# A two-layer graph attention kernel: new order of small steps inside a unit of layer 0, and a shorter reciprocal root

## The chip, the cores and the metric

The kernel runs on one core of a Trainium2 chip. The metric is the device time of one execution in microseconds, lower is better. The kernel before took 1904.17 us as the median of three runs (1901.87 to 1906.42). A profile is one further execution, recorded by the hardware profiler; it took 1750.29 us, and its span from the first to the last instruction is 1748.6 us.

## The reference, cut to what matters

There are 2708 nodes with 1024 features and a sparse 0/1 adjacency matrix (the diagonal is set). Layer 0 is a dot-product graph attention with weights Wf, Wg, W, layer 1 an additive one with W, a1, a2; each is followed by a residual sum and a layer norm.

```python
def _L0_gnn_ref(x, adj, Wf, bf, Wg, bg, W, bW):
    f = x @ Wf + bf
    g = x @ Wg + bg
    e = jax.nn.relu(f @ g.T)
    scores = jnp.where(adj > 0, e, NEG)
    attention = jax.nn.softmax(scores, axis=1)
    return attention @ (x @ W + bW)
...
x = _layernorm(x + _L0_gnn_ref(...))     # layer 0
x = _layernorm(x + _L1_gnn_ref(...))     # layer 1: relu(softmax(mask(leaky_relu(h a1 + (h a2)^T))) h), h = x W
```

## The kernel before, in words

A first stage turns the adjacency rows into lists of neighbours (up to 40 a node), written to the DRAM table `LD`, and multiplies the weights: `M` is the product of Wf and Wg transposed, so a score is a dot product between a neighbour's row of x and a row F = x M of the node itself.

Nodes are sorted by number of neighbours into groups of 32, and four groups make a *unit* of 128 nodes; layer 0 has 22 units (21 full ones and one of a single group). In a unit every group has its own number of tiles; a *tile* is 128 gathered rows of x, four neighbours for each of 32 nodes. Nearly all units have 20 tiles, the last three have 16, 16 and 15.

The ring (L868) has 20 slots of 128 rows. So the tiles of the next unit can be gathered only as the sums of this unit free their slots. Each gather is one indirect DMA on GpSimd's queue.

The loop over units (L1025) does, for unit u, with the work of its neighbours interleaved:

- On TensorE: the weighted sums of u (`lay.sums`, L712), `po` = softmax weights `st` times the gathered rows, then the row totals `pt`, one small matmul a group; transposes of a later unit's x rows (`x_turn`, L902); the product with W of the unit before (into `pm`, residual and norm follow); a small matmul that spreads q; the product F with M of the unit after next (`f_product`, L907); transposes of u's sums `y`.
- On ScalarE: `replicate` (L910) copies F of the next unit into four tiles `Fr`, one for each group, four copies each; the norm of `z` of the unit before; `y` = `po` times the reciprocal of the totals; copies of the transposed tiles.
- On VectorE: `dots` (L916), one dot product of a gathered tile with `Fr`, 20 in a unit, in an order that alternates between groups 0 and 1, then 2 and 3; `soft` (L921, L682), which adds q, masks, takes the maximum, has ScalarE take the exponential, and builds `st` and its row sums `rs`; the residual sum, statistics and root of the unit before (`close`, L932, and `norm`, L604); `q_dot` (L888), one dot of a later unit's x rows; two dots of the normed `z` for layer 1; the reciprocal `ri` of the totals.
- On GpSimd's queue: the 20 ring gathers as slots come free (`gathers`, L669), the scatter of the finished rows to the table of layer 1 (`T<-z`), the load of x rows for a later unit (`load_x`, `xb`), the load of the residual (`load_residual`, L926, into `z`), and four gathers of neighbour lists (`load_lists`, L857, `SL<-LD`) for the unit four ahead.

Each engine executes its instructions in the order in which the program issues them: the class `InOrder` (L61) wraps every engine and binds each instruction behind the one before. That is why almost every line of the profile is L71, the wrapper's line, and why groups are told apart by tile names. Between engines, waits follow from the tiles.

Buffers that matter: `z` (L874), `xb`, `y` and `po` have one buffer, so `z` can be loaded again only when the scatter has read it; transposes and small matmuls share two PSUM buffers `pt` (`ps_t`, L138), so the second of the two x transposes waits until the totals have been read by the reciprocal; products share two buffers `pm`.

`closing` is the generator `close` of the unit before. Its first step (residual sum, statistics, root, shift `sh`) is issued at the end of an iteration, behind `soft` of the next unit. In the next iteration come ScalarE's norm of `z` and its store (second step), the two dots of `z` (third step), and, behind the sums, the scatter. The reciprocal stands at the end of `lay.sums`, so on VectorE it comes behind these dots.

Layer 1 gathers rows of the table T in the same way, in half units, with the same `norm`.

Of the kernel before, what the change touches and what calls it, by code (L numbers as in the profile page):

```python
# [18 lines left out]
EPS = 1e-5  # L19
# [87 lines left out]
def listed_path(ctx, tc, x, adj, Wf, bf, Wg, bg, W, bW, W1, a1, a2, out):  # L107
# [491 lines left out]
    def scatter(table, idx, src):  # L599
        pool.indirect_dma_start(  # L600
            out=table, out_offset=bass.IndirectOffsetOnAxis(ap=idx, axis=0), in_=src,
            in_offset=None, bounds_check=N - 1, oob_is_err=False)

    def norm(z, n, made=None):  # L604


        st = small.tile([P, H, 6], F32, name="bst")
        mv = small.tile([P, 2], F32, name="mv")
        for h in range(H):
            if made is not None:  # L610
                made(h)
            dve.bn_stats(st[:n, h, :], z[:n, h * 512:(h + 1) * 512])
        dve.bn_aggr(mv[:n], st[:n])
        var, r, t = (small.tile([P, 1], F32, name=s) for s in ("var", "rstd", "newton"))
        dve.tensor_scalar(var[:n], mv[:n, 1:2], EPS, None, op0=ALU.add)
        ri, ti = r.bitcast(I32), t.bitcast(I32)
        dve.tensor_scalar(ti[:n], var.bitcast(I32)[:n], 1, None, op0=ALU.logical_shift_right)
        dve.tensor_scalar(ri[:n], ti[:n], -1.0, float(0x5F3759DF), op0=ALU.mult, op1=ALU.add)
        for _ in range(3):
            dve.tensor_scalar(t[:n], var[:n], r[:n], r[:n], op0=ALU.mult, op1=ALU.mult)  # L620
            dve.tensor_scalar(t[:n], t[:n], -0.5, 1.5, op0=ALU.mult, op1=ALU.add)
            dve.tensor_scalar(r[:n], r[:n], t[:n], None, op0=ALU.mult)
        sh = small.tile([P, 1], F32, name="sh")
        dve.tensor_scalar(sh[:n], mv[:n, 0:1], r[:n], -1.0, op0=ALU.mult, op1=ALU.mult)
        yield
        act.activation(z[:n, :D], z[:n, :D], AF.Identity, bias=sh[:n], scale=r[:n])
# [24 lines left out]
    class Layer:  # L651
# [57 lines left out]
            u.rs = small.tile([P, Q], F32, name="rs")  # L709
            dve.tensor_reduce(u.rs[:, :u.G], sc, AX.X, ALU.add)  # L710

        def sums(self, u, po, y):  # L712

            place = lambda k, h: 32 * ((k + 2 * h) % 4)

            def totals():
                pt = ps_t.tile([P, 4, P], F32, name="pt")  # L720
                for h in range(H):
                    for k in range(u.G):
                        j = place(k, h)
                        pe.matmul(pt[j:j + 32, 0, h:h + 1], stack, u.rs[:, k:k + 1], start=True, stop=True)
                return pt

            index = {(k, t): m for m, (k, g, t) in enumerate(u.tiles)}

            queues = []
            for c in range(4):  # L730
                two = [(k, h) for h, k in enumerate((c, (c + 2) % 4)) if k < u.G]
                if c > 1:
                    two.reverse()
                queues.append([(k, h, t) for t in range(u.T) for k, h in two if t < TILES[u.gs[k]]])
            done, halves, pt = 0, {}, None
            while any(queues):
                if pt is None and done >= min(4, u.T):
                    pt = totals()
                now = [q.pop(0) for q in queues if q]
                for k, h, t in now:  # L740
                    j = place(k, h)
                    pe.matmul(po[j:j + 32, h, :], u.st[:, u.col[k, t], :],
                              self.rows(u.at + index[k, t])[:, h * 512:(h + 1) * 512],
                              start=(t == 0), stop=(t == TILES[u.gs[k]] - 1))
                for k, h, t in now:
                    halves[k, t] = halves.get((k, t), 0) + 1
                    if halves[k, t] == H:
                        self.free.add(u.at + index[k, t])
                        self.gathers()
                        done += 1  # L750
            if pt is None:
                pt = totals()
            ri = small.tile([P, H], F32, name="ri")
            spans = [(slice(0, P), slice(0, H))] if u.G == 4 else \
                [(slice(j, j + 32), slice(h, h + 1)) for h in range(H) for j in (place(0, h),)]
            for rows, h in spans:
                dve.reciprocal(ri[rows, h], pt[rows, 0, h])
            for h in range(H):
                rows = slice(0, P) if u.G == 4 else slice(place(0, h), place(0, h) + 32)
                c = slice(h * 512, (h + 1) * 512)  # L760
                act.activation(y[rows, c], po[rows, h, :], AF.Copy, scale=ri[rows, h:h + 1])
# [107 lines left out]
    with ExitStack() as s0s:  # L869
# [10 lines left out]
        def load_x(b):  # L880
            xb[b] = xp.tile([P, D], F32, name="xb") if b > 0 else zs[:, :D]
            gather(pool, xb[b][:nrows[b]], x, ids[:nrows[b], b:b + 1])
# [5 lines left out]
        def q_dot(b):  # L888
            n = nrows[b]
            qs = small.tile([P, 1], F32, name="qs")  # L890
            dot(xb[b][:n], rb, n, qs[:n])
            qd[b] = spread(qs[:n], n, "qd")
# [9 lines left out]
        def x_turn(b):  # L902
            xTs[b] = tp.tile([P, KC, P], F32, name="xT")
            for _ in turn(xb[b], nrows[b], xTs[b]):
                pass
# [4 lines left out]
        def replicate(b, k):  # L910

            Fr[b, k] = frp.tile([P, D], F32, name="Fr")
            for p in range(Q):
                act.copy(Fr[b, k][32 * p:32 * p + 32, :], flat(F[b])[32 * k:32 * k + 32, :])
# [106 lines left out]
        soft(units[0])  # L1021
        for _ in spread2:
            pass
        closing, loaded = iter(()), 3
        for k, u in enumerate(units):  # L1025
            nxt = units[k + 1] if k + 1 < len(units) else None
            b = u.b
            back = seq[k - 1] if k > 0 else None
            ahead = seq[k + 2] if k + 2 < NB else None

            first = k == 0
            po = ps_s.tile([P, H, 512], F32, name="po")
            y[b] = yp.tile([P, D], F32, name="y")
            if back is not None:
                for _ in yTs[back][1]:
                    pass
            reps = list(range(len(nxt.gs))) if nxt is not None and not first else []
            for r in reps[:1]:
                replicate(nxt.b, r)
            next(closing, None)  # L1040
            if loaded is not None:
                q_dot(loaded)
                loaded = None
            next(closing, None)
            for r in reps[1:3]:
                replicate(nxt.b, r)
            if nxt is None:

                for _ in closing:
                    pass  # L1050
                Wp[back] = product(P, yTs.pop(back)[0], Wt, 1)
            lay.sums(u, po, y[b])
            for _ in closing:
                pass
            closing = iter(())
            if ahead is not None and not first:
                x_turn(ahead)
            if k + 3 < NB and not first:
                loaded = seq[k + 3]
                load_x(loaded)  # L1060
            if back is not None and nxt is not None:
                load_residual(back)
                if back > 0:
                    Wp[back] = product(P, yTs.pop(back)[0], Wt, 1)
                else:
                    Wp[back] = whole(split_product(yTs.pop(back)[0], Wt, frp.tile([P, D], F32, name="Fr"), 1))
            if k + 2 == NB:
                load_residual(b)
            spreading = iter(())
            if ahead is not None and not first:  # L1070
                spreading = q_spread(ahead)
                next(spreading)
            for r in reps[3:]:
                replicate(nxt.b, r)
            if ahead is not None and not first:
                f_product(ahead)
            if ahead == NB - 1:
                sp.dma_start(M, W1.rearrange("(k p) d -> p k d", p=P))
            yT = tp.tile([P, KC, P], F32, name="xT")
            steps = turn(y[b], nrows[b], yT, halves=True)  # L1080
            next(steps)
            yTs[b] = yT, steps
            if k + 2 == NB:
                for _ in steps:
                    pass
            if k + 4 < NB and not first:
                load_lists(seq[k + 4])
            if nxt is not None:
                dots(nxt, 0, len(nxt.tiles))
            for _ in spreading:  # L1090
                pass
            if nxt is not None:
                soft(nxt)
            if back is not None:
                closing = close(back)
                next(closing)
# [529 lines left out]
```

## Time and profile before

| what | value |
|---|---|
| median of three runs | 1904.17 us |
| profiled execution | 1750.29 us |
| its span | 1748.6 us |
| 14 full units of layer 0, 405.36 to 975.97 us | 570.61 us |
| one dot of a tile on VectorE | 1.23 us |
| one ring gather on GpSimd's queue, issue | 1.06 us on average |
| one list gather, issue | 1.0 us |
| one replication of F (four copies) on ScalarE | 4.0 us |
| layer 1, from about 1140 us on | 608 us |

A profile line with a time in front is one instruction or several merged ones: start, duration, engine, line, operation, output and input tiles, shapes, count; the bracket is the idle time of the engine before it and what ended it. A line of waits has the engine and tile that waited, what it waited for, the total in us, how often, and the longest. Digits of a clock row are tenths of the full TensorE clock in 40 equal slices. A wait for several things is put down to the last event by time, which may be a chance neighbour.

### The profile page before, as it was taken

How to read it: one execution, taken by the hardware profiler on the slowest of the kernel's cores; microseconds unless marked ns; L12 is line 12 of the kernel's file. 1: busy time of each engine (PE TensorE's matmuls, PEld its weight loads, DVE VectorE, ACT ScalarE, POOL GpSimd, SP SyncE). 2: the span in 40 equal slices, each digit the busy share in tenths (PEclk: the TensorE clock that was granted, in tenths of full speed). 3: DMA queues.
4: the chain of work that ended last, by engine and by line, in shares of the span. 5: the costliest groups of instructions: out<-in, count | busy, mean ns of one | idle time of the engine just before them, and what ended most of it. 6: DMA issues, size and time to landing. Idle time of an engine off the chain costs nothing. (4 is left out here: it accounts for less than half of the span.)

```text
span 1748.6 us, 23112 instructions
## 1 busy us (share of the span) xinstructions
PE 1563.6 (89%) x6969; PEld 675.5 (39%) x6969; DVE 1297.5 (74%) x4262; ACT 643.5 (37%) x902; POOL 1180.9 (68%) x1195
## 2 busy tenths in 40 slices
PE   4999578899999999999999999559899888999896
PEld 2444233344444444444444444213344333343332
DVE  5879846899999989998999977547465555665652
ACT  4555455444444554555554444101111111111111
POOL 7888476467667767776677743177777777777740
PEclk8999778999999999999999999879999999999998
DMA  7656168578877777888887876399999999999960
GB/s 287 228 185 236 38 232 309 199 252 292 302 277 283 269 253 276 294 293 284 303 299 285 291 267 249 121 394 357 367 374 392 391 397 375 384 392 390 396 253 38
DMA packets 149986, 502.80 MB, mean 288 GB/s; under 512 B 32340, under 2 KB 32372, under 8 KB 147144
## 3 DMA queue, kind: packets, MB, share of 16 engines
q0 software_dynamic: 132032, 428.29, 66.2%
q1 hardware_dynamic: 10202, 55.72, 8.4%
q10 hardware_dynamic: 7618, 17.23, 2.7%
q8 instruction: 57, 0.93, 0.2%
q14 instruction: 77, 0.63, 0.1%
HBM read 509.64 MB, written 33.75 MB: 311 GB/s over the span
## 5 line engine op out<-in xcount | busy, mean ns | idle before, releaser
L71 POOL DMA_INDIRECT ring<-in_x_dram,SL x405 | 429.9, 1062 | 164.0 <-issue 70.0
L71 DVE SCALAR_TENSOR_TENSOR j<-ring,Fr 128x1024 bf16<-128x1024 f32 x402 | 493.9, 1229 | 41.1 <-DMA ring<-in_x_dram,SL 13.9
L71 PE MATMUL po<-ring,st 128*32 128x512 f32 x2616 | 324.4, 616 | 56.9 <-ACT y L71 32.5
L71 ACT COPY Fr<-pm 32x1024 f32<-32x1024 f32 (+2 forms) x353 | 340.6, 965 | 18.8 <-PE pm L71 14.1
L71 PE MATMUL pm<-M,yT 128*128 128x512 f32 (+1 forms) x704 | 313.3, 598 | 0.5 <-ACT yT L71 0.5
L71 PE MATMUL pm<-Wt,xT 128*128 128x512 f32 (+1 forms) x704 | 300.5, 599 | 4.7 <-DMA Wt<-in_L_gnn_W_dram 4.7
L71 POOL DMA_INDIRECT ring<-T,SL x249 | 247.0, 992 | 80.5 <-issue 66.3
L71 PE MATMUL pm<-M,xT 128*128 128x512 f32 x672 | 297.5, 601 | 0.0
L71 ACT ACTIVATE scores<-scores 128x12 f32<-128x12 f32 (+9 forms) x65 | 14.0, 216 | 631.6 <-DVE scores L71 631.6
L71 PEld LDWEIGHTS pm<-M,yT 128*128 128x128 f32 (+1 forms) x704 | 127.8, 186 | 185.0 <-issue 183.8
L71 PEld LDWEIGHTS pm<-Wt,xT 128*128 128x128 f32 (+1 forms) x704 | 131.0, 189 | 163.4 <-issue 154.6
L71 PEld LDWEIGHTS pm<-M,xT 128*128 128x128 f32 x672 | 130.2, 194 | 158.0 <-issue 155.1
L71 POOL DMA_INDIRECT more<-T,SL x156 | 154.6, 991 | 48.5 <-issue 43.8
L71 PEld LDWEIGHTS po<-ring,st 128*32 128x32 f32 x2616 | 95.9, 113 | 229.8 <-issue 174.0
L412 POOL TENSOR_TENSOR adj<-adj,iota 128x2708 f32<-128x2708 f32 (+3 forms) x23 | 130.6, 5685 | 22.7 <-ACT adj L71 22.6
L415 DVE MAX8 cand<-adj 128x8 f32<-128x136 f32 (+2 forms) x440 | 97.2, 285 | 37.4 <-POOL adj L412 37.4
L71 PE MATMUL pm<-halfT,WfT 128*128 128x512 f32 x256 | 114.1, 601 | 1.1 <-ACT WfT L71 1.1
L71 POOL DMA_INDIRECT SL<-LD,idq x85 | 86.4, 1016 | 25.8 <-issue 24.0
L71 PE MATMUL po<-more,st 128*32 128x512 f32 x624 | 82.4, 625 | 14.3 <-ACT y L71 14.3
L71 DVE TENSOR_SCALAR scores<-ring,f1q 128x4 f32<-128x4 f32 (+6 forms) x69 | 16.5, 245 | 104.1 <-DMA ring<-T,SL 93.1
L71 POOL DMA_INDIRECT z<-in_x_dram,ids x21 | 24.0, 1142 | 87.1 <-DVE j L71 36.4
L71 PEld LDWEIGHTS pm<-halfT,WfT 128*128 128x128 f32 x256 | 48.2, 193 | 58.0 <-issue 55.2
(214 smaller groups left out, 1539.5 us busy)
## 6 DMA issues: line engine op xcount, KB each, us to landing
adj<-in_adj_dram SPq DMA_DIRECT2D x21, 1354.0 KB, 5.8
X1S<-z SPq DMA_DIRECT2D x19, 512.0 KB, 5.2
ring<-in_x_dram,SL POOLq DMA_INDIRECT x405, 6.5
rows<-in_L_gnn_Wg_dram ACTq DMA_DIRECT2D x8, 512.0 KB, 4.4
rows<-in_L_gnn_Wf_dram ACTq DMA_DIRECT2D x8, 512.0 KB, 3.5
rows<-in_L_gnn_W_dram ACTq DMA_DIRECT2D x8, 512.0 KB, 6.1
Wt<-in_L_gnn_W_dram ACTq DMA_DIRECT2D x1, 4096.0 KB
M<-in_L_gnn_W_dram SPq DMA_DIRECT2D x1, 4096.0 KB
```

The costliest lines, as they stand in the source:

```text
L71: made = self.tc.keep_in_program_order(op(*args, **kwargs))
L412: nc.gpsimd.tensor_tensor(k[:n, cut], k[:n, cut], iota[:n, cut], op=ALU.mult)
L415: nc.vector.max(cand[:n, s, :], k[:n, s * SEG:min((s + 1) * SEG, N)])
```

## The change

Five edits, all in layer 0's loop except the first.

- The reciprocal square root of `norm` becomes a function `rsqrt`: the variance is halved on entry (with the small constant added in the same instruction), the first guess gets a negative sign, and each of the three Newton steps has two instructions instead of three. Both layers use it.
- In `sums`, the reciprocal is issued directly behind the matmuls of the totals, and then `aside()` is called, which issues the norm of `z`, its two dots and the second and third replication. Before, these stood ahead of the call of `sums` and the reciprocal at its end.
- `load_lists` moves from behind the transposes of `y` to between `load_x` and `load_residual`: on GpSimd's queue the four list gathers now come behind the `xb` load and ahead of the `z` load.
- `q_dot` of the loaded x rows moves from the next iteration (behind the residual sum and root) to the end of this one, ahead of the residual sum. The first one, `q_dot(3)`, is issued ahead of the loop.
- The last four dots of the next unit move behind the addition that finishes q of a later unit (`spreading`).

```diff
+    def rsqrt(v, n, scale):
+        half, r, t = (small.tile([P, 1], F32, name=s) for s in ("half", "rstd", "newton"))
+        dve.tensor_scalar(half[:n], v, 0.5 * scale, 0.5 * EPS, op0=ALU.mult, op1=ALU.add)
+        ri, ti = r.bitcast(I32), t.bitcast(I32)
+        dve.tensor_scalar(ti[:n], half.bitcast(I32)[:n], 1, None, op0=ALU.logical_shift_right)
+        dve.tensor_scalar(ri[:n], ti[:n], -1.0, float(0x5F3759DF - 0x400000 - (1 << 31)), op0=ALU.mult, op1=ALU.add)
+        for _ in range(3):
+            dve.tensor_scalar(t[:n], half[:n], r[:n], r[:n], op0=ALU.mult, op1=ALU.mult)
+            dve.tensor_scalar(r[:n], t[:n], 1.5, r[:n], op0=ALU.subtract, op1=ALU.mult)
+        return r
...
-        dve.tensor_scalar(var[:n], mv[:n, 1:2], EPS, None, op0=ALU.add)
...
-        for _ in range(3):
-            dve.tensor_scalar(t[:n], var[:n], r[:n], r[:n], op0=ALU.mult, op1=ALU.mult)
-            dve.tensor_scalar(t[:n], t[:n], -0.5, 1.5, op0=ALU.mult, op1=ALU.add)
-            dve.tensor_scalar(r[:n], r[:n], t[:n], None, op0=ALU.mult)
+        r = rsqrt(mv[:n, 1:2], n, 1.0)
...
             def totals():
...
-                return pt
+                spans = ...
+                for rows, h in spans:
+                    dve.reciprocal(ri[rows, h], pt[rows, 0, h])
+                aside()
...
-            for rows, h in spans:
-                dve.reciprocal(ri[rows, h], pt[rows, 0, h])
...
-            next(closing, None)
-            if loaded is not None:
-                q_dot(loaded)
-                loaded = None
-            next(closing, None)
-            for r in reps[1:3]:
-                replicate(nxt.b, r)
...
+            def aside():
+                next(closing, None)
+                next(closing, None)
+                for r in reps[1:3]:
+                    replicate(nxt.b, r)
+
+            lay.sums(u, po, y[b], aside)
...
                 load_x(loaded)
+            if k + 4 < NB and not first:
+                load_lists(seq[k + 4])
             if back is not None and nxt is not None:
                 load_residual(back)
...
-            if k + 4 < NB and not first:
-                load_lists(seq[k + 4])
             if nxt is not None:
-                dots(nxt, 0, len(nxt.tiles))
+                dots(nxt, 0, max(0, len(nxt.tiles) - 4))
             for _ in spreading:
                 pass
             if nxt is not None:
+                dots(nxt, max(0, len(nxt.tiles) - 4), len(nxt.tiles))
                 soft(nxt)
+            if loaded is not None:
+                q_dot(loaded)
+                loaded = None
             if back is not None:
                 closing = close(back)
                 next(closing)
```

More of the change, by code (lines that the diff above doesn't have):

```diff
@@ L613, in norm @@
         dve.bn_aggr(mv[:n], st[:n])
-        var, r, t = (small.tile([P, 1], F32, name=s) for s in ("var", "rstd", "newton"))
-        dve.tensor_scalar(var[:n], mv[:n, 1:2], EPS, None, op0=ALU.add)
-        ri, ti = r.bitcast(I32), t.bitcast(I32)
-        dve.tensor_scalar(ti[:n], var.bitcast(I32)[:n], 1, None, op0=ALU.logical_shift_right)
-        dve.tensor_scalar(ri[:n], ti[:n], -1.0, float(0x5F3759DF), op0=ALU.mult, op1=ALU.add)
-        for _ in range(3):
-            dve.tensor_scalar(t[:n], var[:n], r[:n], r[:n], op0=ALU.mult, op1=ALU.mult)
-            dve.tensor_scalar(t[:n], t[:n], -0.5, 1.5, op0=ALU.mult, op1=ALU.add)
-            dve.tensor_scalar(r[:n], r[:n], t[:n], None, op0=ALU.mult)
+        r = rsqrt(mv[:n, 1:2], n, 1.0)
         sh = small.tile([P, 1], F32, name="sh")
@@ L710, in soft, with sums @@
             dve.tensor_reduce(u.rs[:, :u.G], sc, AX.X, ALU.add)
-        def sums(self, u, po, y):
+        def sums(self, u, po, y, aside):
             place = lambda k, h: 32 * ((k + 2 * h) % 4)
+            ri = small.tile([P, H], F32, name="ri")
             def totals():
@@ L724, in totals @@
                         pe.matmul(pt[j:j + 32, 0, h:h + 1], stack, u.rs[:, k:k + 1], start=True, stop=True)
-                return pt
+                spans = [(slice(0, P), slice(0, H))] if u.G == 4 else \
+                    [(slice(j, j + 32), slice(h, h + 1)) for h in range(H) for j in (place(0, h),)]
+                for rows, h in spans:
+                    dve.reciprocal(ri[rows, h], pt[rows, 0, h])
+                aside()
             index = {(k, t): m for m, (k, g, t) in enumerate(u.tiles)}
@@ L734, in sums @@
                 queues.append([(k, h, t) for t in range(u.T) for k, h in two if t < TILES[u.gs[k]]])
-            done, halves, pt = 0, {}, None
+            done, halves, summed = 0, {}, False
             while any(queues):
-                if pt is None and done >= min(4, u.T):
-                    pt = totals()
+                if not summed and done >= min(4, u.T):
+                    summed = True
+                    totals()
                 now = [q.pop(0) for q in queues if q]
@@ L750, in sums @@
                         done += 1
[L751 to L755, printed above, removed]
-            for rows, h in spans:
-                dve.reciprocal(ri[rows, h], pt[rows, 0, h])
+            if not summed:
+                totals()
             for h in range(H):
@@ L1023, in listed_path @@
             pass
-        closing, loaded = iter(()), 3
+        closing = iter(())
+        q_dot(3)
         for k, u in enumerate(units):
@@ L1051, in listed_path @@
                 Wp[back] = product(P, yTs.pop(back)[0], Wt, 1)
-            lay.sums(u, po, y[b])
+            def aside():
[4 more added lines that the diff above has]
+            lay.sums(u, po, y[b], aside)
             for _ in closing:
@@ L1092, in listed_path @@
             if nxt is not None:
+                dots(nxt, max(0, len(nxt.tiles) - 4), len(nxt.tiles))
                 soft(nxt)
+            if loaded is not None:
+                q_dot(loaded)
+                loaded = None
             if back is not None:
```

## The prediction

> **What bounds the kernel now.** I read the page's clock row first, then busy time cut at successive starts of `st` (VectorE, once per unit), then the waits of each engine between 405.36 and 975.97 us, then the timeline of one unit.
>
> ```profile
> span 1748.6 us, 23112 instructions
> ...
> PE 1563.6 (89%) x6969; PEld 675.5 (39%) x6969; DVE 1297.5 (74%) x4262; ACT 643.5 (37%) x902; POOL 1180.9 (68%) x1195
> ...
> PEclk8999778999999999999999999879999999999998
> ```
>
> Busy time by unit (PE, PEld, DVE, ACT, POOL, clock, DMA share):
>
> ```profile
> 732.24:772.86 40.62, 39.62 (x186) 17.26 (x185) 37.15 (x82) 20.77 (x25) 28.74 (x28) 1.00 0.81 290
> 772.86:813.90 41.04, 39.95 (x187) 17.35 (x184) 37.28 (x83) 20.77 (x26) 28.74 (x28) 1.00 0.80 282
> 813.90:854.61 40.71, 38.69 (x177) 16.57 (x178) 37.35 (x82) 20.73 (x25) 27.32 (x28) 1.00 0.80 292
> ```
>
> The 14 units between 405.36 and 975.97 take 570.61 us, 40.76 us each, at full clock. TensorE and VectorE both look full. The waits tell which pays (us in total, times, longest):
>
> ```profile
> DVE j L71 <- DMA ring<-in_x_dram,SL: 11.4, 20, 1.2
> DVE z L71 <- DMA z<-in_x_dram,ids: 4.9, 11, 1.3
> DVE st L71 <- ACT scores L71: 4.3, 15, 0.3
> DVE j L71 <- ACT Fr L71: 4.2, 14, 0.3
> PE pt L71 <- DVE ri L71: 10.3, 12, 2.0
> PE po L71 <- DVE st L71: 5.1, 8, 1.0
> ```
>
> VectorE has no slack: 37.3 us recorded busy, 1.8 us of named waits per unit (24.8/14), and the rest is spacing between short instructions. TensorE waits 15.4/14 = 1.1 us per unit, always for VectorE. So VectorE's order is the loop that sets the unit. One unit on GpSimd, ScalarE, VectorE and TensorE:
>
> ```profile
> 804.23 1.02 POOL L71 DMA_INDIRECT T<-z,ids  x1 [0.30 <-issue]
> 805.55 1.03 POOL L71 DMA_INDIRECT xb<-in_x_dram,ids  x1 [0.30 <-issue]
> 810.96 0.99 POOL L71 DMA_INDIRECT z<-in_x_dram,ids  x1 [4.38 <-DVE q L71]
> 812.25 1.00 POOL L71 DMA_INDIRECT SL<-LD,idq  x1 [0.30 <-issue]
> ...
> 817.46 0.99 POOL L71 DMA_INDIRECT ring<-in_x_dram,SL  x1 [0.30 <-issue]
> ```
> ```profile
> 779.85 1.24 ACT L71 ACTIVATE z<-z,sh,rstd 128x1024 f32<-128x1024 f32 x1 [1.84 <-DVE sh L71]
> 781.11 8.12 ACT L71 COPY Fr<-pm 32x1024 f32<-32x1024 f32 x8
> ```
> ```profile
> 785.20 1.22 DVE L71 SCALAR_TENSOR_TENSOR j<-ring,Fr 128x1024 bf16<-128x1024 f32 x1 [0.31 <-ACT Fr L71]
> ```
> ```profile
> 783.76 0.66 PE L71 MATMUL pt<-ident,xb 128*128 128x128 f32 x4 [0.52 <-DVE ri L71]
> 1027.44 1.11 PE L71 MATMUL pt<-ident,xb 128*128 128x128 f32 x4 [3.14 <-DVE ri L71]
> ```
>
> GpSimd idles 4.38 us before `z`, then spends 5.2 us on lists, and only then refills the ring. ScalarE cannot make the second `Fr` before it has normed `z`, so VectorE's second dot waits about 0.3 us in every unit.
>
> [...] 59.0 us of idle in 14 units before the `z` gather, 4.2 each, behind the scatter that reads `z` (`DVE q` there is only the event nearest in time). [...] Here a 128x1 operation takes 0.15 to 0.28 us. [...]
>
> **The change, part by part, per unit.** S is the start of `st`.
>
> *Shorter root.* It drops the middle operation of three Newton steps: pitch 777.67 to 777.86, 0.19 us each, so 0.57. The new last operation has two scalars instead of one; bounds are 0 (as 0.21) and 0.06 each (as `newton<-var,rstd`, 0.27). I take half: −0.48 us. `half` replaces `var` at equal price.
>
> *Lists between scatter and residual.* From the scatter's start: 1.32 to `xb`, 1.33 past it, 4 × 1.30 lists, so `z` goes out at scatter + 7.85 instead of + 6.6 (mean of 14; 4.2 to 7.8), its landing wait covered. Four small list transfers move ahead of it in the same queue. GpSimd is then free before the next S. The first ring gather falls from S + 3.4 to S + 2.24 (`po` at S + 0.88, first slot freed 1.36 later, as 1016.50 to 1017.86 shows where GpSimd was idle). The ring, hence the scatter, is 1.15 us earlier: scatter S + 29.8 (mean of before 30.95), `z` S + 37.7, landed 4.3 to 5.1 us later (851.50 to 855.75, 931.66 to 936.77): 1.4 to 2.2 us after the next S, for a unit near 40.5.
>
> *q's dot ahead of the residual sum.* Its 1.39 us (779.74 to 781.13, with `qd`) now starts at S + 0.82, so the sum starts at S + 2.2, just after `z` lands: the 0.35 us wait (4.9/14) is covered. `xb` is in by about 1.5 us before it. But the same 1.39 us no longer stands between `sh` and the second dot, where it hid ScalarE. `Fr` is ready 5.35 us after ScalarE starts on `z` (779.85 to 785.20). After `sh` VectorE now has only reciprocal, two `z` dots and one dot. The `Fr` wait grows from 0.3 to about 1.7 us: +1.39 us. Nothing else can run, since the dots stand behind it in order.
>
> *Ring waits.* The dots after the second come later against S by 1.39 − 0.48 − 0.35 = 0.56 us and the ring 1.15 us earlier, 1.7 us of slack against a longest ring wait of 1.2: −0.81 us (11.4/14). If gathers are paced by transfer rate rather than issue, part stays.
>
> *Reciprocal behind its matmuls.* It moves from S + 10.7 to about S + 7.8, before the two `z` dots. It waits for `pt` matmuls done at S + 2.9. TensorE's second transposes come at S + 10.2, so its wait goes. That frees TensorE (its own work is 39.42 us: `po` to first transposes 8.85, 0.5, then 30.07 to the next `po`), but TensorE then waits about 1 us for `st` instead: zero while VectorE sets the unit, up to −0.7 us (10.3/14) otherwise. Moving q's addition ahead of the last four dots only reorders 0.14 us; its matmul is done 6 us before.
>
> *Sum per unit:* −0.48 − 0.35 − 0.81 + 1.39 = −0.25 us; with 0.05 left for late `z`, −0.2 us. Over 14 units: −3 us (bounds +8, if the ring waits stay, and −19, if TensorE's 39.42 is reached).
>
> *Outside the steady stretch.* At 1027.44 TensorE waits 3.14 us for the reciprocal because the residual came late; the next lines ran slow (granted clock 0.91 in 1020 to 1040; product 14.72 against 13.90, bias 1.06 against 0.59). With the root shorter and q's dot and the `z` dots off the path, the reciprocal falls near 1023.0, before the transposes at 1024.1. TensorE is unbroken from there to 1095, so −4.5 us reaches the end (at least −2). The roots at 1121 and 1735 lie on the chain: −1 us.
>
> Sum −8.5: the profiled execution (1750.29 us, span 1748.6 and 1.7 around it) would take 1741.8. The runs have a median of 1904.17, 154 us above it, and no view shows why. I carry the difference over unchanged: 1904.2 − 8.5 = 1895.7. No change means within 0.2% (3.8 us).
>
> **Rivals.**
> A. *Nothing measurable.* The 154 us may be a slower TensorE. [...] VectorE's waits vanish in slack. Then only the roots remain: 1903. For it: no other excess is seen; against: the stage profiled ran at 1.00.
> B. *More than worked.* If the runs' excess lies in transfers, the ring's earlier start counts fully, or the unit reaches TensorE's 39.42: 14 × 1.34 = 19, with 5.5 outside: 1880. Against: the `Fr` wait.
> C. *Slower.* A later `z` delays `sh`, `Fr` and every dot one for one. It lands 0 to 0.8 us ahead of the sum, so a slip of 0.8 + 0.2 + 5.5/14 = 1.4 us breaks even; four list transfers ahead of it, or a scatter landing late, could do it. At 2.5 us: 14 × 1.1 = +15: 1919. The same holds if `Fr` is later than worked. For it: `z` issue times vary by 3.6 us. Against: transfers are few there.
>
> **Chances.** As worked (gain 2 to 15) 0.40, of which 0.09 is under 3.8 us; A 0.22; B 0.13; C 0.25. Faster 0.31 + 0.13 = 0.44, same 0.09 + 0.22 = 0.31, slower 0.25. The range 1883 to 1912 holds the first two, half of B and most of C up to +0.4%. The likeliest case alone: 1889 to 1902.
>
> **What would show it.** Right: `DVE j <- ACT Fr` near 1.7 us per unit; ring and `z` waits nearly gone; no `PE pt <- DVE ri`; `PE po <- DVE st` near 1 us per unit; first ring gather at S + 2.2; units near 40.5 us. Wrong: `DVE z <- DMA z` above 1 us (C), units at 39.5 (B), or units unchanged with the 1027 wait still there.

## The result, and the profile after

The change made the kernel slower: 1975.93 us as the median of four runs (1971.22 to 1984.69) against 1905.3 us (1901.87 to 1909.23), a ratio of 1.039, 95% interval 1.0348 to 1.0432. The profiled execution took 1971.22 us, its span is 1969.5 us. Where a ratio below is not that of the medians, disturbed runs were left out of it.

The page of the changed kernel (span, busy time, clock in 40 slices):

```profile
span 1969.5 us, 22958 instructions
...
PE 1643.3 (83%) x6947; PEld 690.5 (35%) x6969; DVE 1269.4 (64%) x4130; ACT 649.1 (33%) x902; POOL 1179.1 (60%) x1195
...
PEclk9999679699999999898989899769989999999989
```

Busy time by unit, cut at the starts of `st`, in the columns of the prediction (PE, PEld, DVE, ACT, POOL, clock, DMA share, GB/s):

```profile
734.68:776.51 41.83, 40.91 (x181) 17.58 (x182) 37.05 (x81) 20.74 (x25) 28.60 (x27) 0.96 0.75 261
776.51:826.17 49.66, 40.97 (x167) 16.82 (x169) 36.93 (x82) 20.76 (x25) 27.82 (x27) 0.86 0.67 246
826.17:869.99 43.82, 42.87 (x196) 19.15 (x195) 36.97 (x80) 20.75 (x25) 27.84 (x27) 1.00 0.74 260
869.99:919.54 49.55, 37.09 (x158) 14.78 (x160) 36.72 (x79) 20.85 (x25) 27.68 (x27) 0.83 0.66 243
```

Before, the 14 units took 39.8 to 41.8 us. Now units of 41.5 to 43.8 us mostly alternate with units of 49.3 to 49.7 us (one takes 56.8), while VectorE and GpSimd have no more work than before. The waits between 402.38 and 1108.81 us say who stands still:

```profile
POOL ring L71 <- PE po L71: 134.3, 17, 30.6
DVE q L71 <- remote: 77.7, 10, 11.1
...
PE pm L71 <- issue: 44.7, 44, 2.2
```

VectorE waits at q's addition, which needs a small matmul of TensorE and now stands ahead of the last four dots (`remote` means that the profile finds no engine to name); and TensorE waits at the product with M for nothing that the profile shows (`issue`). The timeline of one long unit, GpSimd first:

```profile
804.93 0.99 POOL L71 DMA_INDIRECT ring<-in_x_dram,SL  x1 [0.30 <-issue]
806.22 1.02 POOL L71 DMA_INDIRECT T<-z,ids  x1 [0.30 <-issue]
807.54 1.03 POOL L71 DMA_INDIRECT xb<-in_x_dram,ids  x1 [0.30 <-issue]
808.88 1.00 POOL L71 DMA_INDIRECT SL<-LD,idq  x1 [0.31 <-issue]
...
814.09 0.99 POOL L71 DMA_INDIRECT z<-in_x_dram,ids  x1 [0.30 <-issue]
```

TensorE and VectorE in the same stretch:

```profile
801.48 0.28 PE L71 MATMUL pt<-qd,rep 128*128 128x4 f32 x2
...
805.98 0.59 PE L71 MATMUL pm<-M,xT 128*128 128x512 f32 x1 [1.51 <-issue]
808.11 1.01 PE L71 MATMUL pm<-M,xT 128*128 128x512 f32 x1 [1.55 <-issue]
...
814.43 1.01 PE L71 MATMUL pm<-M,xT 128*128 128x512 f32 x1 [1.09 <-issue]
816.56 1.01 PE L71 MATMUL pm<-M,xT 128*128 128x512 f32 x1 [1.11 <-issue]
817.96 11.05 PE L71 MATMUL pm<-M,xT 128*128 128x512 f32 x22 [0.39 <-issue]
```
```profile
818.16 0.22 DVE L71 TENSOR_SCALAR q<-pt,s 128x4 f32<-128x4 f32 x1 [9.36 <-remote]
```

The mechanics that the prediction listed are all there: `z` leaves at scatter + 7.87, the lists stand between, the ring starts early. What it did not have is a *slow stretch* of TensorE: from about 803 to 817.3 us one pair of weight load and matmul takes some 2.1 us (805.98 to 808.11, 814.43 to 816.56) instead of 0.43. It ends 2.1 us after GpSimd has issued its last transfer of the unit, at scatter + 11.0 us, and so it does in four other units (scatter + 10.9 to + 11.0: 591.4, 910.5, 1008.1 and 1099.8 us). q's matmul is recorded at 801.48, ahead of the slow stretch, and yet VectorE, idle for 9.36 us, gets its result only at 818.16, 0.9 us after the stretch: it also holds back what TensorE had just been recorded as doing.

The granted clock is not what starts it. It is still 1.00 in the first 4 us and then falls (0.50 from 808 to 817 us); that adds to the cost until it is back (PE, PEld, DVE, ACT, POOL, clock, DMA share, GB/s):

```profile
803.00:807.00 4.00, 1.67 (x4) 0.47 (x3) 3.90 (x7) 0.00 (x0) 3.09 (x4) 1.00 1.01 410
808.00:817.00 9.00, 4.49 (x5) 1.14 (x4) 0.81 (x2) 0.00 (x0) 5.56 (x6) 0.50 0.57 186
821.00:826.00 5.00, 5.00 (x13) 2.24 (x12) 4.53 (x18) 0.08 (x1) 0.00 (x0) 1.00 0.00 0
```

In the trace of after, between 540 and 1100 us, the weight loads sort the units. In the eight whose GpSimd queue has no pause of 1 us or more from the first ring gather to `z` (some 36 us) the stretch costs 0.7 to 12.7 us (sum of the gaps over 0.9 us, less 0.24 each); in the five with one pause of 1.0 to 1.4 us in the middle of the ring it costs nothing (the unit ahead of these, with a pause of 1.4 us, lost 1.9 us). Before, GpSimd always paused ahead of `z`, 4.2 us on average, waiting for the scatter, and then took the lists; the change fills that pause, and GpSimd pauses behind `z` instead, where it waits for free slots.

The profile shown before (1750.29 us) has no such stretch, and it was 154 us faster than the runs. The runs below fell on four chips. On two of them the kernel before takes about 1748 us, as in that profile; on the other two about 1900 us, as in the runs shown. I call them the *first kind* and the *second kind* of chip. By its time the profile before came from the first kind and the change was judged on the second. Whether the kind belongs to the chip itself or to something else that was going on there isn't shown.

### The profile page after: what moved, and what is told of

The parts are those of the page before. It is cut to its first block, busy times and chain, and to the rows that moved or that the text cites. A ratio compares the mean times of both kernels' runs of the same rounds, so it can differ in the third digit from the quotient of the medians.

```text
span 1969.5 us, 22958 instructions
## 1 busy us (share of the span) xinstructions
PE 1643.3 (83%) x6947; PEld 690.5 (35%) x6969; DVE 1269.4 (64%) x4130; ACT 649.1 (33%) x902; POOL 1179.1 (60%) x1195
## 5 line engine op out<-in xcount | busy, mean ns | idle before, releaser
L71 PE MATMUL po<-ring,st 128*32 128x512 f32 x2616 | 347.6, 630 | 97.1 <-issue 33.0
L71 PE MATMUL pm<-M,xT 128*128 128x512 f32 x672 | 327.9, 637 | 44.8 <-issue 44.3
L71 PE MATMUL pm<-M,yT 128*128 128x512 f32 (+1 forms) x704 | 318.2, 602 | 5.3 <-issue 4.2
L71 PEld LDWEIGHTS pm<-M,xT 128*128 128x128 f32 x672 | 136.6, 204 | 228.5 <-issue 225.8
L71 ACT ACTIVATE y<-po,ri 128x512 f32<-128x512 f32 (+1 forms) x88 | 58.1, 684 | 247.5 <-remote 115.0
L71 PE MATMUL po<-more,st 128*32 128x512 f32 x624 | 98.3, 666 | 18.8 <-issue 18.1
L71 PE MATMUL pt<-ident,y 128*128 128x128 f32 (+1 forms) x352 | 52.5, 273 | 23.2 <-issue 19.2
L71 ACT COPY xT<-pt 128x512 f32<-128x512 f32 (+2 forms) x109 | 48.2, 499 | 69.1 <-PE pt L71 58.4
```

Source lines behind the costliest of these rows:

```text
L71: made = self.tc.keep_in_program_order(op(*args, **kwargs))
```

## The experiments

Three theories at first. **Q**: q's addition, moved ahead, holds VectorE. **L**: the lists between scatter and residual. **R**: the reciprocal with what now hangs on it. Each of these edits of the change was undone by itself, and the kernel before was run once more with a profile.

**Before, unchanged.**

> The kernel before, unchanged, for a profile taken beside the others. Its timed runs (1902 to 1909 us) are some 155 us above its one profiled execution (1750.29 us). If the slow stretches of TensorE that the changed kernel's trace shows (one weight load and one matmul every 2.1 us, waiting for nothing recorded) belong to the chip's surroundings and not to the change, this run shows them too and its span is near 1900. If they come from the change, its span is near 1750 and its trace has none. Ratio 1.00 either way.

**q's addition behind all dots again.**

```diff
-                dots(nxt, 0, max(0, len(nxt.tiles) - 4))
+                dots(nxt, 0, len(nxt.tiles))
             for _ in spreading:
                 pass
             if nxt is not None:
-                dots(nxt, max(0, len(nxt.tiles) - 4), len(nxt.tiles))
                 soft(nxt)
```

> The changed kernel with q's addition back behind all dots of the next unit. Theory Q (VectorE is held at q's addition, with the last four dots queued behind it): 1900 to 1915 us, the wait of q gone and units near 41 to 43 us. Theory L (the lists ahead of the residual load) and theory R (the reciprocal and the steps moved with it): still 1960 to 1980.

**Lists behind the residual again** (where they stood before).

```diff
                 load_x(loaded)
-            if k + 4 < NB and not first:
-                load_lists(seq[k + 4])
             if back is not None and nxt is not None:
                 load_residual(back)
 ...
+            if k + 4 < NB and not first:
+                load_lists(seq[k + 4])
             if nxt is not None:
                 dots(nxt, 0, max(0, len(nxt.tiles) - 4))
```

> The changed kernel with the four list gathers back behind the residual load. Theory L: 1900 to 1920 us. Theory Q: 1960 to 1980, with q still waiting 8 us in every other unit. Theory R: 1960 to 1980.

**Reciprocal at the end of the sums again**, and the norm of `z`, its dots and the two replications ahead of the sums.

```diff
-                for rows, h in spans:
-                    dve.reciprocal(ri[rows, h], pt[rows, 0, h])
-                aside()
+                return pt, spans
 ...
+            for rows, h in spans:
+                dve.reciprocal(ri[rows, h], pt[rows, 0, h])
             for h in range(H):
 ...
+            next(closing, None)
+            next(closing, None)
+            for r in reps[1:3]:
+                replicate(nxt.b, r)
             if nxt is None:
 ...
```

> The changed kernel with the reciprocal back at the end of the sums, and the norm of z, its dots and two replications back ahead of the sums. Theory R: 1900 to 1920 us. Theories Q and L: 1960 to 1980.

Measured on a chip of the second kind: before 1897.12 us (ratio to the other runs of before 0.9981, 0.9952 to 1.0011); without q's move 1943.95 (1.0219, 1.0141 to 1.0298); without the lists' move 1911.57 (1.0068, 1.0028 to 1.0107); without the reciprocal's 1973.64 (1.0288, 1.0195 to 1.038). By the ranges R and Q fall and L stands. The changed kernel did not run beside these four; when it ran on this chip later (below) it took 1925.37 us, so only the lists' kernel comes out below it, and no gain from undoing q's move or the reciprocal's is shown. But the trace of the lists' kernel spoke against L as "four more transfers in the way": slow stretches of 4.5 us and more are left in four of its units, and in each of the four they end at scatter + 2.4 to + 4.7 us, soon after GpSimd's pause ahead of `z` begins (scatter + 2.4). What the lists had done was to fill that pause. So theory **P**: TensorE slows down when GpSimd issues its transfers without a break for too long.

The profile of before on this chip (span 1897.9 us) has units of 43 us instead of 40.8, with GpSimd's pause in its place and a second one at the third ring gather, so that at most 20 transfers follow each other without a break. From 428 to 990 us it has no slow stretch; the product goes through in one piece:

```profile
774.84:817.82 42.98, 41.27 (x181) 18.00 (x182) 37.14 (x82) 20.78 (x26) 29.41 (x27) 1.00 0.78 268
```
```profile
771.73 0.99 POOL L71 DMA_INDIRECT z<-in_x_dram,ids  x1 [4.28 <-DVE j L71]
...
782.24 1.90 POOL L71 DMA_INDIRECT ring<-in_x_dram,SL  x1 [1.69 <-DVE sh L71]
```
```profile
802.77 13.89 PE L71 MATMUL pm<-M,xT 128*128 128x512 f32 x32
```

Neither half of the expectation came true: the time of the second kind is there almost without slow stretches. So the second kind is slower for some other reason, and the slow stretches of the changed kernel come on top.

**A break put in, nothing else moved.** Ten fills of a small scratch tile between the tenth and eleventh ring gather of each unit. They took 3.2 us in the trace, more than the 2 us that the expectation gave them.

```diff
 ...
+                if self.rest is not None and m > 2 * self.count and m - u.at == 10:
+                    for _ in range(10):
+                        pool.memset(self.rest, 0.0)
                 idx = SL[:, g, t:t + 1] if m >= self.count else SL0[:, self.first[g], t:t + 1]
                 gather(pool, self.rows(m), self.table, idx)
```

> The changed kernel, with ten small fills of a scratch tile (about 2 us, no transfer) put between the tenth and eleventh ring gather of each unit on GpSimd's queue; nothing else is moved. Theory P (TensorE is slowed when GpSimd issues transfers without a break from the first ring gather to the residual, 36 us): the break ends it, no pair of weight load and matmul takes 2.1 us any more, units all near 42 us, 1900 to 1930 us. Theory L (the four list transfers between scatter and residual, or the late residual, cost the time): nothing changes or 2 us a unit are added, 1965 to 2010 us.

**The lists' move alone**, in the kernel before.

```diff
                 load_x(loaded)
+            if k + 4 < NB and not first:
+                load_lists(seq[k + 4])
             if back is not None and nxt is not None:
                 load_residual(back)
 ...
-            if k + 4 < NB and not first:
-                load_lists(seq[k + 4])
             if nxt is not None:
                 dots(nxt, 0, len(nxt.tiles))
```

> The kernel before with the move of the four list gathers alone. Theory P: GpSimd's pause of 4 us ahead of the residual is gone, so runs of gathers without a break appear and with them the slow stretches of TensorE in part of the units: 1920 to 1960 us. The rival, that the move does harm only together with q's addition ahead of the last dots: 1890 to 1908 us.

**q's addition ahead alone**, in the kernel before (the first diff of this section the other way round).

> The kernel before with q's addition ahead of the last four dots alone. Theory P: TensorE has no slow stretches here, its matmul for q is done long before, so 1893 to 1908 us. The rival, that the order of VectorE alone is the loss: 1920 to 1945 us.

**Lists and q's addition both back**: the changed kernel with its first and second diff above.

> The changed kernel with two of its edits undone: the lists again behind the residual, and q's addition again behind all dots. What is left is the shorter root, the reciprocal behind its matmuls and q's dot ahead of the residual sum. Theory P: GpSimd pauses ahead of the residual again, so most slow stretches go: 1890 to 1908 us. The rival, that the reciprocal or q's dot cost time of their own: 1912 to 1940 us.

These runs fell on a chip of the first kind (before: 1747.9 us), and most expectations, which were for the second, missed. The lists alone took 1739.7 us (0.9961, 0.9944 to 0.9977): faster. q's addition alone 1749.3 (1.0012, 1.0001 to 1.0022). Both back 1742.28 (0.9967, 0.9956 to 0.9978). The ten fills 1781.41 (1.0209, 1.0173 to 1.0246): a cost. In the trace of the lists alone GpSimd runs from the first ring gather to `z` without a pause and waits only after it; TensorE goes through the same product in one piece:

```profile
722.71:762.58 39.87, 39.38 (x182) 17.14 (x182) 37.36 (x82) 20.77 (x25) 27.64 (x27) 1.00 0.81 293
762.58:802.80 40.22, 39.38 (x182) 17.14 (x182) 37.37 (x82) 20.77 (x25) 27.99 (x27) 1.00 0.81 291
```
```profile
759.68 1.00 POOL L71 DMA_INDIRECT z<-in_x_dram,ids  x1 [0.30 <-DVE j L71]
764.99 0.99 POOL L71 DMA_INDIRECT ring<-in_x_dram,SL  x1 [4.30 <-PE po L71]
```
```profile
748.94 13.89 PE L71 MATMUL pm<-M,xT 128*128 128x512 f32 x32
```

So an unbroken run of GpSimd is not enough by itself; it takes the second kind of chip too. Four kernels were therefore run again, the changed one with them.

> The changed kernel unchanged, on whichever chip this turns out to be: one on which the kernel before takes about 1748 us, or one on which it takes about 1900. Theory P (TensorE's slow stretches need both GpSimd's unbroken run of gathers and what makes the second chip slow): on the first chip no slow stretch, units of 40 to 41 us, 1735 to 1750 us, so no loss; on the second, alternating units and 1965 to 1985 us. The rival, that the new order itself costs time: about 4% more than before on either, 1810 or more on the first.

> The kernel before with the move of the four list gathers alone, again. On a chip where the kernel before takes about 1900 us theory P expects slow stretches of TensorE in part of the units and 1920 to 1960 us, where the other chip gave 0.4% less than before; the rival, that this move is harmless by itself there too, 1885 to 1900 us. On a chip of the first kind: 1735 to 1745 us under both.

> The changed kernel with 2 us of small fills in the middle of each unit's ring gathers, again. On a chip where the kernel before takes about 1900 us theory P expects that the break ends the slow stretches: units near 43 us, 1900 to 1930 us. The rival (lists or late residual cost the time): 1965 to 2010 us. On a chip of the first kind 1775 to 1790 us under both, as measured.

> The changed kernel with the lists again behind the residual and q's addition again behind all dots, again. On a chip where the kernel before takes about 1900 us theory P expects 1885 to 1908 us, since GpSimd pauses ahead of the residual as before; the rival, that the reciprocal or q's dot cost time of their own, 1912 to 1940 us. On a chip of the first kind about 1742 us.

This chip was of the second kind (before: 1900.4 us). Changed 1932.0 us (1.0253, 1.0033 to 1.0473). Lists alone 1953.85 (1.0296, 0.9955 to 1.0637; its four runs, 1927.08 to 1977.95, lie all above the seven of before, 1865.5 to 1907.43). Ten fills 1899.89 (1.0106, 0.9937 to 1.0275; its runs, 1894.55 to 1900.12, lie all below those of the changed kernel, 1913.82 to 1949.84). Both back 1904.45 (1.0126, 0.9951 to 1.03). By the medians of all runs the four ratios are 1.017, 1.028, 1.000 and 1.002; the intervals of the last three include 1, so what these three show rests on the runs that don't overlap and on the traces. The lists alone and both back lie in P's ranges, the ten fills at the lower edge of theirs, and the changed kernel, 1932 us, below the 1965 to 1985 expected. The lists alone, faster on the other chip, have slow stretches here, with TensorE and then GpSimd:

```profile
752.78 0.59 PE L71 MATMUL pm<-Wt,xT 128*128 128x512 f32 x1 [1.55 <-issue]
754.90 0.59 PE L71 MATMUL pm<-Wt,xT 128*128 128x512 f32 x1 [1.53 <-issue]
757.01 1.01 PE L71 MATMUL pm<-Wt,xT 128*128 128x512 f32 x1 [1.52 <-issue]
```
```profile
785.98 1.00 POOL L71 DMA_INDIRECT ring<-in_x_dram,SL  x1 [19.91 <-PE po L71]
```

That stretch lies in the product with W, ahead of the one with M: it isn't bound to one product. Next, TensorE is late with `po`, no slot comes free, and GpSimd waits 19.91 us. With the ten fills none of the 17 units from 400 us on has a slow stretch.

**Shorter breaks.** The same edit with five fills (1.6 us), and with five fills and q's addition behind all dots; the changed kernel beside them.

> The changed kernel unchanged. Theory P: on a chip where the kernel before takes about 1748 us TensorE has no slow stretches, units of 40 to 41 us and 1735 to 1750 us, no loss; where it takes about 1900 us, alternating units and 1925 to 1985 us. The rival, that the new order itself costs time: 1790 us or more on the first kind of chip too.

> The changed kernel with five small fills (about 1 us) instead of ten in the middle of each unit's ring gathers. Theory P: pauses of 1.2 us in the trace were enough to keep a unit free of slow stretches, so where the kernel before takes about 1900 us this takes 1885 to 1915 us, about 10 to 15 us less than with 2 us if the fills themselves delay the ring; where it takes about 1748 us, 1745 to 1770 us. The rival, that 2 us are needed: 1930 us or more on the slower kind of chip.

> The changed kernel with q's addition again behind all dots and five small fills (about 1 us) in the middle of each unit's ring gathers. Theory P: with no slow stretches the place of q's addition is worth nothing, so within 5 us of the kernel with the five fills alone. The rival, that q's place costs time of its own: 10 us or more less.

Again the second kind (before: 1896.94 us). Changed 1925.37 us (1.0164, 1.0059 to 1.0269). Five fills 1862.43 (0.9816, 0.974 to 0.9893). Five fills without q's move 1864.92 (0.9819, 0.9735 to 0.9902). The break, as GpSimd's queue has it, the product in one piece, and TensorE's wait at its products, 44.7 us in 44 places in the changed kernel's first trace (here between 428 and 972 us, 13 units):

```profile
690.99 1.57 POOL L71 MEMSET rest<- 128x200 f32 x5
```
```profile
700.34 13.90 PE L71 MATMUL pm<-M,xT 128*128 128x512 f32 x32
```
```profile
PE pm L71 <- issue: 2.2, 6, 0.4
```

1.6 us of nothing but fills in each unit take 63 us off the changed kernel, and it then beats the kernel before by 1.8%. The place of q's addition is worth nothing once TensorE isn't slow (2.5 us between the two, inside their spread): q's 77.7 us of waiting were the slow stretch seen from VectorE. The five fills came out below P's range (1885 to 1915 us); on the first kind, below, the same kernel only equals the kernel before, and why it beats it here isn't shown.

**The changed kernel on the first kind of chip**, with five fills and with two (0.6 us) beside it.

> The changed kernel unchanged, once more. Theory P: on a chip where the kernel before takes about 1748 us no slow stretch of TensorE and 1735 to 1750 us; where it takes about 1900 us, slow stretches and 1920 to 1985 us. The rival, that the new order itself costs time: 1790 us or more on the first kind of chip too.

> The changed kernel with five small fills (1.6 us) in the middle of each unit's ring gathers, once more. Theory P: where the kernel before takes about 1900 us, 1850 to 1875 us as measured; where it takes about 1748 us there is nothing to win by the break, and the ring comes 1 to 2 us later, so 10 to 25 us more than the changed kernel, 1745 to 1770 us.

> The changed kernel with two small fills (about 0.6 us) in the middle of each unit's ring gathers. Theory P: if the length of the break counts, 0.6 us leaves part of the slow stretches where the kernel before takes about 1900 us: 1875 to 1930 us; if any break is enough, 1845 to 1865 us. Where it takes about 1748 us: between the changed kernel and the one with five fills.

This time the first kind (before: 1748.84 us). The changed kernel takes 1735.31 us, 0.9928 (0.9905 to 0.9951): it is *faster* here. Five fills 1748.63 (1.0002, 0.9991 to 1.0013), two 1736.2 (0.9935, 0.9915 to 0.9955). The break costs 13 us where there is nothing to win. Whether two fills would be enough on the second kind stays open, since these runs did not fall there.

**All traces together.** Take as a run the transfers that GpSimd issues without an idle time of 0.9 us or a fill between them, and as a slow stretch three or more gaps over 0.9 us between weight loads. Between 400 and 1090 us the twelve traces of the second kind, by their time, have 44 runs of 26 or 27 transfers, and 35 come with a slow stretch; of 37 runs of 20 to 25 transfers 12 do, of 299 shorter ones 1. All 48 slow stretches end within 3 us of the last transfer of their run. In the eight traces of the first kind none of 74 runs of 20 or more has one.

## Why the prediction was wrong

The forecast was 1895.7 us, the result 1975.93. Its steps hold on the first kind of chip, from which, by its time, its profile came, and fail where it carried them.

*On the first kind of chip* the changed kernel shows what was forecast. Three units, and the waits between 406.71 and 970.33 us (14 units, 563.62 us):

```profile
729.40:769.54 40.14, 39.20 (x181) 17.19 (x182) 36.76 (x79) 20.75 (x26) 27.93 (x27) 1.00 0.78 287
769.54:809.70 40.16, 39.25 (x182) 17.17 (x182) 36.79 (x80) 20.75 (x26) 27.73 (x27) 1.00 0.80 290
809.70:849.84 40.14, 39.22 (x182) 17.18 (x182) 36.76 (x79) 20.76 (x26) 27.79 (x27) 1.00 0.80 294
```
```profile
DVE j L71 <- ACT z L71: 17.3, 14, 1.3
...
PE po L71 <- DVE st L71: 12.1, 13, 1.4
...
DVE j L71 <- ACT Fr L71: 4.2, 14, 0.3
...
DVE z L71 <- DMA z<-in_x_dram,ids: 0.3, 1, 0.3
DVE j L71 <- DMA ring<-in_x_dram,SL: 0.2, 1, 0.2
```

| step of the sum, per unit | worked out | shown |
|---|---|---|
| shorter root (statistics to `sh`, 4.37 to 3.80 us) | −0.48 | −0.57 |
| wait for `z` (4.9 to 0.3 us in 14 units) | −0.35 | −0.33 |
| ring waits (11.4 to 0.2 us) | −0.81 | −0.80 |
| `Fr` wait (4.2 to 17.3 + 4.2 us) | +1.39 | +1.24 |
| sum; unit 40.76 to 40.26 us | −0.25 | −0.46; −0.50 |

The two rows that wait for ScalarE are one thing: the dot behind `z` and `Fr` waits 1.5 us a unit, where 1.7 was forecast. TensorE's wait for the reciprocal is gone, its wait for `st` is 0.86 us a unit (about 1 forecast), the first ring gather leaves at S + 2.0 to 2.2. The last units, with the wait of 3.14 us at 1027, shrink from 115.23 to 110.13 us (from the last of the 14 units to the start of `st` at 1091.20, now 1080.46): −5.1 where −4.5 was forecast. The rest of the span to its end gives −2.7 where the roots were to give −1, and the start is 1.4 us later. Together −13.4 us of span against the forecast −8.5.

*The step that failed* is the last of the sum: "The runs have a median of 1904.17, 154 us above it, and no view shows why. I carry the difference over unchanged." The sum held that the change would act on the slower runs as on the profile. Part of the difference does carry over: layer 1 takes 690.2 us in the kernel before on the second kind (602.9 on the first) and 689.3 in the changed one:

```profile
1280.20:1969.50 689.30, 576.29 (x2502) 226.89 (x2502) 322.83 (x1571) 92.87 (x195) 418.81 (x506) 0.93 0.84 306
```

But ahead of layer 1 the changed kernel takes 72.5 us more (1280.2 against 1207.7), where the sum had some −7.5. There TensorE is slowed by a pattern in GpSimd's queue, and the change makes that pattern. The kernel before is protected by a pause (4.28 us in its trace there) that the prediction counted as plain idle time: "GpSimd idles 4.38 us before `z`", then "GpSimd is then free before the next S", booked as a gain of 1.15 us.

*q's addition*: "its matmul is done 6 us before" is right on the first kind. On the second the slow stretch holds back its result, and VectorE waits 8 to 11 us for it in the long units.

*The rivals.* A asked whether the runs' TensorE is slower, by an amount that no view showed, and answered that VectorE's waits would then vanish in its slack. It was close in the place and wrong in the kind: not a lower clock throughout (1.00 at the start of a slow stretch), but stretches that the order on another engine brings about. C foresaw "slower", by a late `z`; in the result VectorE waits for the transfer of `z` only twice between 402 and 1109 us (2.9 us in all), so C's mechanism is not what happened. B's 24 us are not reached: the 13.5 us of the first kind of chip lie between it and the forecast.

*What stays open* is why GpSimd's run slows TensorE, why on some chips or at some times only, and why the kernel before, almost without slow stretches, is slower there. One explanation, a guess of mine, is that TensorE gets its instructions late. The page of the changed kernel lists two DMA queues of the kind "instruction" for the whole run (57 packets, 0.93 MB, so 16 KB each, and 76 packets, 0.62 MB), but not which engine they serve. And in a slow stretch of the changed kernel (720.2 to 725.2 us) all that the DMA queues moved between 722 and 724 us is this:

```profile
DMA packets 38, 0.01 MB, mean 3 GB/s; under 512 B 38, under 2 KB 38, under 8 KB 38
## 3 DMA queue, kind: packets, MB, share of 16 engines
q0 software_dynamic: 38, 0.01, 3.9%
```

No instruction packet was under way, and the queues were nearly empty while TensorE still took 2.1 us a pair. In the long stretch from 803.5 to 817.3 us there was no instruction packet either, but there the queues were 71.8% busy. So a late instruction packet behind busy queues doesn't explain the short stretch; what else it is isn't shown. GpSimd's waiting for something and GpSimd filling a tile both broke the run (0.56 us of idle follow the fills), so it is the issuing of transfers (or the transfers) rather than a busy GpSimd that goes with the slow stretch.

## What to carry to other kernels

A gap between a profile and the timed runs is a finding, not an offset: before working out microseconds from a profile, get one whose time is that of the runs. An idle stretch on an engine off the critical path can still be holding something up (here GpSimd's 4 us ahead of `z`); before filling it, ask what else happens in it. When one engine crawls with nothing to wait for, look at what the other queues do from start to end of that stretch, and test by putting a break into one of them.

## What the runs showed of the hardware

- The same program takes 1748 to 1749 us on two chips and 1897 to 1900 us on two others. Of the difference between the two profiles of the kernel before, 87 us lie in layer 1, which takes 602.9 us on the first and 690.2 us on the second from its first sum on:

```profile
1145.70:1748.60 602.90, 534.59 (x2502) 219.62 (x2502) 345.06 (x1636) 88.05 (x195) 419.45 (x506) 0.96 0.91 350
```
```profile
1207.70:1897.90 690.20, 575.01 (x2502) 224.33 (x2502) 331.81 (x1636) 93.16 (x195) 420.55 (x506) 0.93 0.85 306
```

- On the second kind, TensorE fell to one pair of weight load and matmul in about 2.1 us instead of 0.43, at a cost of 0.7 to 12.7 us a unit in the changed kernel's trace, when GpSimd had issued indirect transfers about every 1.3 us, for 22 to 33 us in seven stretches of that trace, without a break; it recovered within 3 us of GpSimd's last transfer of the run, in all 48 slow stretches of the twelve traces. On the first kind none of 74 runs of 20 or more transfers had a slow stretch. With fills of 1.6 us in the middle of the run (a memory fill of 128x200 takes 0.26 us) TensorE's longest wait at its products was 0.4 us in 13 units. In the long slow stretch shown the granted clock was 1.00 for the first 4 us and fell to 0.50 later.
